# A fifth resident group of image rows, in the room of offset weights, half of the beside weights and one accumulator

## The chip, the cores and the metric

The kernel runs on one core of one Trainium2 chip. The metric is device time of one execution, in microseconds; lower is better. Three runs of the kernel before took 4093.18, 4094.98 and 4102.82 us; their median is 4094.98 us.

## The reference

The input `x` has two images of 256 channels and 128 x 128 points, in f32. Two layers follow each other, each added to its input:

1. `x1 = x + deform_conv(gn(x))`. `gn` is a group normalisation over groups of 8 channels. A 3x3 convolution of `gn(x)` gives 27 values at each point: for each of the nine taps an offset in y, an offset in x and a mask (after a sigmoid). Each tap is sampled at its shifted position by bilinear interpolation of four corners, multiplied by its mask, and the nine samples are contracted with `w_conv` (256 x 256 x 9), plus a bias.
2. `out = x1 + sum over 8 experts of p_e * conv_3x1(conv_1x3(gn(x1)))`. Each expert has 8 hidden channels, so together there are 64 hidden channels; the expert's probability is folded into the hidden values.

```
y0 = floor(py); x0 = floor(px); wy = py - y0; wx = px - x0
v00 * (1 - wy) * (1 - wx) + v01 * (1 - wy) * wx + v10 * wy * (1 - wx) + v11 * wy * wx
```

## The kernel before, in words

**Tables.** For each image a table in device memory holds normalised `x` with points as rows. One row of 4096 bytes at a point's address covers all four corners of an interpolation, because a cell holds two neighbouring rows of the image. Sampling one tap for one row of 128 points is then one gather of 128 such rows.

**Units and slots.** The middle of the program, the stream, is a sequence of 2304 units, 1152 for each image (`UPI`): 16 groups of 8 rows (`GR`), two chunks of 4 rows each, 9 taps, 4 rows. A loop over slots writes the order by hand. Slot `s` issues, for different units: the gather of unit `s + 15` (`GA`, POOL's queue), the product of unit `s + 3` (ScalarE: corner 1 times its weight into an accumulator, L564), the three remaining corners (VectorE, L570), the convolution matmul of unit `s - 8` (TensorE, L595), two transposes of unit `s - 1` (L580) and, in every second slot, the copy of two transposed units out of PSUM (`keep`, ScalarE, L588). Everything else is a piece put at a slot of its own with `put(slot, piece)`. A group is 72 slots. Engines work through their own instructions in this order, and SP's DMAs also go out in order: a DMA that waits for a buffer holds up those behind it.

**Groups of x.** A group is a tile of [128, 2, 1024] f32. Image tiles live in three buffers used in rotation (`XB`, pool `x`) and in `XR` = 4 further ones (pool `x_stay`). `x_tile` (L278) chooses: the last `XR` groups of an image, and the first `XR` of image 0, take the latter. `stays` (L285) says which groups keep their result in SBUF for the second layer: the last `XR` of image 0, the last `XR + XB` of image 1. The results of other groups are stored to `x1` (L611) and read back by the experts (L726). `load_x` (L531) loads group g + 1 at slot 72 g - 54, in the case of image 0 only from the group on that the head has not kept.

**Head.** All 16 groups of image 0 are loaded, their statistics taken, and its table is written. Groups 0 to `XB + XR - 1` stay in SBUF. `offset_pieces` (L206) then makes the weights of the offset convolution with the normalisation folded in: `wus` is `wu` times 1/deviation; `spread`, two matmuls and nine shifted matmuls give the constants of the shift; `at` holds base positions for the first, the middle and the last group. There is one set of `wus` and of the three `at` for each image.

**Stream, image 0.** Beside the units, `table_beside` (L614) makes image 1's table. A first pass reads image 1 for statistics: one chunk (512 KB) every 10 slots, and the last `XR` groups as whole tiles in `x_stay`, each when the group of image 0 that held the buffer has been stored. Norm pieces and image 1's `offset_pieces` follow. A second pass goes backwards over the 32 chunks: load unless still resident (L623, L627), normalise (ScalarE, L654), transpose, copy, and store 1 MB of table rows (L203). Its step is 21 slots; a load stands 20 slots ahead of its normalise. `offsets_of` (L300) computes gather indices and weights of each group some 83 slots ahead of its first unit.

**Stream, image 1.** The second layer for image 0 (`experts`, L710) runs beside image 1's units, one chunk every 33 slots, from the last chunk backwards. **Tail:** the second layer for image 1, 16 groups from the last backwards, nothing beside it.

**Second layer.** `back` (L757) multiplies hidden rows that pair up in the 128 partitions, with two of the four slots of `wout`; `back_beside` (L767) uses half of the partitions of the two other slots, whose other halves are zero.

**Accumulators.** The product's accumulators come from a pool of 9 (`acc`, L510).

Of the kernel before, what the change touches and what calls it, by code (L numbers as in the profile page):

```python
# [31 lines left out]
F32 = mybir.dt.float32  # L32
I32 = mybir.dt.int32
AF = mybir.ActivationFunctionType
ALU = mybir.AluOpType
# [3 lines left out]
P = 128  # L39
B, C, H, W = 2, 256, 128, 128  # L40
NH = C // P
# [3 lines left out]
NO = 3 * K2  # L45
NX = 3 * NO
NU = 3 * NX
# [3 lines left out]
GR = 8  # L51
# [6 lines left out]
ER = 64  # L58
# [3 lines left out]
UPG = UPC * CPG  # L62
UPI = UPG * NG
UNITS = B * UPI
GA = 15
# [1 line left out]
TL = 1  # L67
KL = 2
LM = 8
XB, XR = 3, 4  # L70


@with_exitstack
def layers(ctx, tc, x, w_om, b_om, w_cv, b_cv, w_in, w_out, probs, out):
    nc = tc.nc
# [5 lines left out]
    cp = ctx.enter_context(tc.tile_pool(name="const", bufs=1))  # L81
# [7 lines left out]
    idp = cp.tile([P, P + 2], F32, name="idp")  # L89
# [19 lines left out]
    base = cp.tile([P, GR, NO], F32, name="base")  # L109
# [13 lines left out]
    bias = cp.tile([P, NO], F32, name="bias")  # L123
    bcv = cp.tile([P, NH], F32, name="bcv")
    pr = cp.tile([P, 1], F32, name="pr")
    wu = cp.tile([P, NH, 3, 3, NO], F32, name="wu")
    win = cp.tile([P, NH, 3, ER], F32, name="win")

    wout = cp.tile([P, 4, C], F32, name="wout")
    nc.gpsimd.memset(wout, 0.0)  # L130
    wcv = cp.tile([P, NH, K2, C], F32, name="wcv")

    def frame(b):
# [69 lines left out]
        nc.sync.dma_start(cells(b, y + r, n), pairs)  # L203


    def offset_pieces(norm, oc, psum, tag, name):  # L206
        mean, rstd, shift = norm
        wus = oc.tile([P, NH, 3, NX], F32, name=f"wus_{name}")
        at = [oc.tile([P, GR, NO], F32, name=f"at{i}_{name}") for i in range(3)]
        spread = oc.tile([P, NH, P], F32, tag="spread", name=f"spread_{name}")  # L210
        nb = oc.tile([P, NU], F32, tag="nb", name=f"nb_{name}")
        by_row = oc.tile([P, 3, NO], F32, tag="by_row", name=f"by_row_{name}")
        ps = {}

        def scale(h):
            w = wu[:, h].rearrange("p y x o -> p (y x o)")
            nc.vector.tensor_scalar(
                wus[:, h].rearrange("p y o -> p (y o)"), w, rstd[:, h : h + 1], None, ALU.mult
            )

        def spread_out():
            nc.vector.tensor_copy(spread, shift.unsqueeze(2).broadcast_to([P, NH, P]))

        def constant():
            ps[0] = psum.tile([P, 512], F32, tag=tag, name=f"ps_nb_{name}")
            for h in range(NH):
                nc.tensor.matmul(
                    ps[0][:, :NU], lhsT=spread[:, h], rhs=wu[:, h].rearrange("p y x o -> p (y x o)"),
                    start=(h == 0), stop=(h == NH - 1),
                )  # L230

        def shifted():
            ps[1] = psum.tile([P, 512], F32, tag=tag, name=f"ps_at_{name}")
            for ty in range(3):
                for tx in range(3):
                    at_ = (2 - ty) * NX + tx * NO
                    nc.tensor.matmul(
                        ps[1][:, ty * NO : (ty + 1) * NO], lhsT=idp[:, tx : tx + P],
                        rhs=nb[:, at_ : at_ + NO], start=(tx == 0), stop=(tx == 2),
                    )  # L240

        def rows(t):
            return by_row[:, t].unsqueeze(1).broadcast_to([P, GR, NO])

        pieces = [
            lambda: scale(0),
            lambda: scale(1),
            spread_out,
            constant,
            lambda: nc.vector.tensor_copy(nb, ps[0][:, :NU]),  # L250
            shifted,
            lambda: nc.vector.tensor_copy(
                by_row.rearrange("p t o -> p (t o)"), ps[1][:, : 3 * NO]
            ),
            lambda: nc.vector.tensor_tensor(
                at[1], base, bias.unsqueeze(1).broadcast_to([P, GR, NO]), ALU.add
            ),
            lambda: nc.vector.tensor_tensor(at[1], at[1], rows(0), ALU.add),
            lambda: nc.vector.tensor_tensor(at[1], at[1], rows(1), ALU.add),
            lambda: nc.vector.tensor_tensor(at[1], at[1], rows(2), ALU.add),  # L260

            lambda: nc.vector.tensor_copy(at[0], at[1]),
            lambda: nc.vector.tensor_copy(at[2], at[1]),
            lambda: nc.vector.tensor_sub(at[0][:, 0], at[0][:, 0], by_row[:, 0]),
            lambda: nc.vector.tensor_sub(at[2][:, GR - 1], at[2][:, GR - 1], by_row[:, 2]),
        ]
        return (wus, at), pieces

    def pool(stack, name, bufs, **kw):
        return stack.enter_context(tc.tile_pool(name=name, bufs=bufs, reuse_waits="tile", **kw))  # L270
# [17 lines left out]
    stream = ExitStack()  # L288
# [4 lines left out]
    p_m = pool(stream, "p_m", 3, space=PSUM)  # L293
    norms0, offs = [None] * B, [None] * B
# [125 lines left out]
    with ExitStack() as s:  # L420
# [24 lines left out]
        nc.sync.dma_start(bcv, b_cv)  # L445
        nc.sync.dma_start(wcv, w_cv)
        nc.sync.dma_start(win, w_in)
        for i, (even, odd) in enumerate(((1, 2), (None, 0), (0, 1), (2, None))):
            for half, t in enumerate((even, odd)):
                if t is not None:  # L450
                    nc.sync.dma_start(wout[half * ER : (half + 1) * ER, i], w_out[:, t])
        for half in range(2):
            nc.sync.dma_start(pr[half * ER : (half + 1) * ER], probs)
        for b in range(B):
# [4 lines left out]
        mean, rstd, shift = norms0[0]  # L459
# [20 lines left out]
        for g in range(NG):  # L480
# [4 lines left out]
            for i in range(0, GR, 2):  # L485
                ps = ht.tile([P, 2, C], F32, tag="t", name=f"hpt_{g}_{i}")
# [20 lines left out]


    gp = pool(stream, "gather", GA)
    ap = pool(stream, "acc", 9)  # L510
    sp = pool(stream, "sampled", 3)
    st = pool(stream, "stat", 1)
    p_o = pool(stream, "p_o", 1, space=PSUM)
    p_t = pool(stream, "p_t", 3, space=PSUM)
    oc = pool(stream, "offs", 1)
    offs[0], pieces = offset_pieces(norms0[0], oc, p_m, "m", "0")
    for piece in pieces:
        piece()
    sides = ExitStack()
    stream.enter_context(sides)  # L520
# [5 lines left out]
    def put(slot, piece, opens=False):  # L526
        sched[slot].append(piece)
        if opens:
            opened.add(slot)
# [84 lines left out]
    def table_beside(b):  # L614
        xq = pool(sides, "tx", 2)
        pq = pool(sides, "tpx", 2)
        held = {}
# [3 lines left out]
        def load(j, what):  # L621
            held[what, j] = xq.tile([P, NH, N], F32, tag="tx", name=f"{what}_{b}_{j}")
            nc.sync.dma_start(held[what, j], xv[:, :, j * N : (j + 1) * N])  # L623

        def load_group(g, what):
            xt = held[what, "g", g] = x_tile(b, g, what)
            nc.sync.dma_start(xt, xv[:, :, g * GN : (g + 1) * GN])  # L627
            if g < XB:
                xts[b, g] = xt
# [41 lines left out]
        slot = 4  # L671
        for j in range(NCH):
            g, i = divmod(j, CPG)
            if g < NG - XR:
                put(slot, lambda j=j: load(j, "xs"))
            elif i == 0:

                slot = max(slot, UPG * (g - NG + XR + 1) + LM + 12)
# [6 lines left out]
        for piece in pieces:  # L685
            put(slot, piece)
            slot += 2
        offs[b], pieces = offset_pieces(norms0[b], oc, p_m, "m", str(b))
        for n, piece in enumerate(pieces):
            put(slot + 2 * n, piece)  # L690
        slot -= 12
        for j in range(NCH - 1, -1, -1):
            g, i = divmod(j, CPG)
            if g < XB and i == CPG - 1:
                put(slot, lambda g=g: load_group(g, "xt"))
            elif XB <= g < NG - XR:
                put(slot, lambda j=j: load(j, "xt"))
            for h in range(NH):
                put(slot + 20 + 3 * h, lambda j=j, h=h: normalise(j, h))
            put(slot + 24, lambda j=j: start(j))  # L700
            for n, i in enumerate(range(0, CR, 2)):
                put(slot + 26 + 4 * n, lambda j=j, i=i: turn_rows(j, i))
                put(slot + 28 + 4 * n, lambda j=j, i=i: keep_rows(j, i))
            put(slot + 33, lambda j=j: store_cells(b, CR * j, held["px", j], 0, CR))
            slot += 21
        put(slot + 13, store_top)
        return slot + 14

# [1 line left out]
    def experts(b, norm, pools, psums, put_, rows, order, first, step, ahead, early=0):  # L710
# [3 lines left out]
        xs, ns, hs, ps = {}, {}, {}, {}  # L714
        _, rstd, shift = norm
        n, nj = rows * W, rows // 2
# [50 lines left out]
        def back_beside(ci):  # L767


            own, edge = slice(0, (nj - 1) * W), slice((nj - 1) * W, nj * W)  # L770
            low, rest = slice(0, W), slice(W, nj * W)
            parts = [(0, ci, rest, own), (1, ci, own, rest), (0, ci - 1, low, edge), (1, ci + 1, edge, low)]
            parts = [part for part in parts if 0 <= part[1] < count]
            for m in range(NH):
                for i, (t, c, to, of) in enumerate(parts):
                    half = slice(ER, P) if t == 0 else slice(0, ER)
                    nc.tensor.matmul(  # L777
                        ps[t][:, m, to], lhsT=wout[half, 1 + 2 * t, m * P : (m + 1) * P],
                        rhs=hs[c][half, of], start=False,
                        stop=(banks or m == NH - 1) and all(part[0] != t for part in parts[i + 1 :]),  # L780
                    )
# [14 lines left out]
        for i in range(count + 1):  # L796
            e = first + step * i
# [7 lines left out]
            if i > 0:  # L805
# [4 lines left out]
                at_ = e + 22  # L810
# [15 lines left out]
    for G in range(B * NG):  # L826
        b, g = divmod(G, NG)
        slot = UPG * G
# [12 lines left out]
    slot = UPI + LM + 10  # L841
# [18 lines left out]
    while s < end or any(t >= s for t in sched):  # L860
# [9 lines left out]
        if when(s - LM):  # L870
            u = s - LM
            apply_tap(u)
            b, ci, k, i = unit(u)
            if k == K2 - 1 and i % NH == NH - 1:
                m = i // NH
# [69 lines left out]
```

## Time and profile before

| | us |
|---|---|
| median of the runs | 4094.98 |
| the profiled execution's own time | 3743.08 |
| its span, first to last instruction | 3741.3 |
| stream of image 0, about | 156 to 1895 |
| second pass of image 1's table, first to last store issued | 745 to 1739 |
| stream of image 1, about | 1895 to 3550 |
| tail, to the end | 3550 to 3741 |

One execution was profiled; all views are of it. It is 352 us shorter than the median of the runs. Busy time of an engine is a sum over its instructions; the granted clock of TensorE is given as a share of full speed, and its mean is 0.980. A group's row reads: line, engine, operation, output <- inputs, shapes, count, busy us and mean ns of one, then the idle time ahead of these instructions and what ended most of it.

### The profile page before, as it was taken

Reading aid. Unit: us, or ns where it says so; the run is one execution under the profiler, and the core shown is the slowest. Engines: PE = TensorE matmul, PEld = TensorE weight load, DVE = VectorE, ACT = ScalarE, POOL = GpSimd, SP = SyncE. Lnnn points to the kernel's source line nnn. Section 1 sums busy time; section 2 is a strip of 40 time slices with the busy share of each in tenths; the row PEclk is TensorE's granted clock in tenths of the full one; section 3 lists DMA queues with packets and bytes.
Section 4 is the critical chain, followed back from the end, with each engine's and each line's share of the span. In section 5 each row is a group of like instructions: output and inputs, shape, how many; then the busy total and the mean of one; then the engine's idle time right before and its main releaser. Section 6 shows DMA issues by size and latency. Waiting matters only on the chain. (4 is left out here: it accounts for less than half of the span.)

```text
span 3741.3 us, 51320 instructions
## 1 busy us (share of the span) xinstructions
PE 3379.1 (90%) x13916; PEld 1799.5 (48%) x13916; DVE 3354.6 (90%) x7922; ACT 1918.1 (51%) x3883; POOL 2381.9 (64%) x2337
## 2 busy tenths in 40 slices
PE   3688889999888888889999999999999999999999
PEld 2444444444444444444444555555555555555433
DVE  6499999999888889899999999999999999999812
ACT  2355544555555555555555555555555555555432
POOL 0377666667666667667777766777777677776400
PEclk9699999999999999999999999999999999999999
DMA  9999999999999999999999999999999999999743
GB/s 358 376 407 405 399 400 390 379 395 412 406 400 410 409 406 396 410 397 398 395 390 393 400 387 410 400 403 403 399 407 403 400 409 392 409 404 387 294 150 120
DMA packets 421960, 1431.71 MB, mean 383 GB/s; under 512 B 41726, under 2 KB 45482, under 8 KB 421546
## 3 DMA queue, kind: packets, MB, share of 16 engines
q0 software_dynamic: 331776, 1208.11, 82.0%
q1 hardware_dynamic: 89898, 220.33, 15.4%
q8 instruction: 113, 1.85, 0.2%
q14 instruction: 173, 1.42, 0.1%
HBM read 1302.40 MB, written 125.87 MB: 382 GB/s over the span
## 5 line engine op out<-in xcount | busy, mean ns | idle before, releaser
L570 DVE SCALAR_TENSOR_TENSOR acc<-g,wt,acc 128x256 f32<-128x256 f32 x6912 | 2966.7, 481 | 151.4 <-ACT acc L564 82.7
L554 POOL DMA_INDIRECT g<-table,cidx x2304 | 2371.0, 1029 | 1007.6 <-DVE acc L570 391.9
L595 PE MATMUL po<-sm,wcv 128*128 128x512 f32 x4608 | 2404.5, 604 | 162.6 <-ACT sm L588 84.0
L564 ACT ACTIVATE acc<-g,wt 128x256 f32<-128x256 f32 x2304 | 1120.3, 507 | 806.4 <-DMA g<-table,cidx 656.2
L580 PEld LDWEIGHTS ptr<-idp,acc 128*128 128x128 f32 x4608 | 607.2, 142 | 1459.7 <-issue 726.1
L588 ACT COPY sm<-ptr 128x512 f32<-128x512 f32 x1152 | 664.8, 577 | 728.7 <-PE ptr L580 727.0
L580 PE MATMUL ptr<-idp,acc 128*128 128x128 f32 x4608 | 909.1, 279 | 92.9 <-DVE acc L570 71.7
L595 PEld LDWEIGHTS po<-sm,wcv 128*128 128x128 f32 x4608 | 725.5, 192 | 221.8 <-ACT sm L588 112.4
L321 PE MATMUL pu<-wus,x 128*128 128x81 f32 (+2 forms) x1448 | 261.0, 306 | 0.0
L321 PEld LDWEIGHTS pu<-wus,x 128*128 128x128 f32 x1448 | 208.5, 193 | 1.9
L748 PE MATMUL ph<-xcn,win 128*64 128x254 f32 (+3 forms) x1152 | 177.8, 458 | 3.1 <-ACT xcn L731 3.1
L762 PE MATMUL pe<-h,wout 128*128 128x256 f32 (+1 forms) x384 | 125.5, 456 | 1.1 <-DVE xc L786 1.1
L786 DVE TENSOR_TENSOR xc<-pe,xc 128x512 f32<-128x512 f32 x84 | 55.1, 684 | 73.2 <-issue 70.8
L748 PEld LDWEIGHTS ph<-xcn,win 128*64 128x64 f32 x1152 | 79.0, 138 | 81.3 <-issue 51.5
L755 ACT ACTIVATE h<-ph,pr 128x256 f32<-128x256 f32 (+1 forms) x48 | 26.3, 547 | 138.2 <-PE ph L748 138.1
L604 DVE SCALAR_TENSOR_TENSOR x<-po,bcv,x 128x512 f32<-128x512 f32 x116 | 86.6, 747 | 8.1 <-PE po L595 8.1
L786 DVE TENSOR_TENSOR x<-pe,x 128x512 f32<-128x512 f32 x44 | 28.3, 683 | 71.7 <-PE pe L777 71.7
L762 PEld LDWEIGHTS pe<-h,wout 128*128 128x128 f32 x384 | 66.8, 190 | 39.8 <-issue 36.4
L608 DVE BATCH_NORM_STATS2 stats<-x 128x6 f32<-128x512 f32 x116 | 79.7, 687 | 0.1
L491 DVE COPY hpx<-hpt 128x512 f32<-128x512 f32 x32 | 21.1, 687 | 57.0 <-DMA table<-hpx 46.0
L777 PE MATMUL pe<-h,wout 64*128 64x128 f32 (+1 forms) x752 | 69.3, 321 | 0.0
L777 PEld LDWEIGHTS pe<-h,wout 64*128 64x128 f32 x752 | 51.8, 187 | 25.6 <-issue 16.9
(102 smaller groups left out, 845.9 us busy)
## 6 DMA issues: line engine op xcount, KB each, us to landing
g<-table,cidx POOLq DMA_INDIRECT x2304, 9.3
table<-tpx SPq DMA_DIRECT2D x32, 1024.0 KB, 11.3
table<-hpx SPq DMA_DIRECT2D x15, 2048.0 KB, 9.4
x<-in_x_dram SPq DMA_DIRECT2D x29, 1024.0 KB, 12.6
out_dram<-xc SPq DMA_DIRECT2D x42, 512.0 KB, 7.7
x<-x SPq DMA_DIRECT2D x18, 1024.0 KB, 10.3
xs<-in_x_dram SPq DMA_DIRECT2D x24, 512.0 KB, 8.3
xc<-x SPq DMA_DIRECT2D x24, 512.0 KB, 8.5
```

What stands on the lines that cost most here:

```text
L321: nc.tensor.matmul(held["ps", j][:, lo:hi], lhsT=xt[:, h, r * W : (r + 1) * W], rhs=w[:, lo - i + 2 : hi - i + 2], start=(i == 2 and h == ...
L554: nc.gpsimd.indirect_dma_start(out=gt[:], out_offset=None, in_=tables[b][:, :], in_offset=bass.IndirectOffsetOnAxis(ap=idx[:, rr, k : k + ...
L564: nc.scalar.activation(acc, gts[u][:, 0:C], AF.Copy, scale=wt[:, 0, rr, k : k + 1])
L570: nc.vector.scalar_tensor_tensor(accs[u], gt[:, q * C : (q + 1) * C], wt[:, q, rr, k : k + 1], accs[u], ALU.mult, ALU.add)
L580: nc.tensor.transpose(pts[u // 2][:, h, (r % 2) * W : (r % 2 + 1) * W], acc[:, h * P : (h + 1) * P], ident)
L588: nc.scalar.copy(sms[u // CR][:, :, (r - 1) * W : (r + 1) * W], pts.pop(u // 2))
L595: nc.tensor.matmul(pos_[b, ci, m], lhsT=wcv[:, h, k, m * P : (m + 1) * P], rhs=sms[u // CR][:, h], start=(k == 0 and h == 0), stop=(k == K ...
L604: nc.vector.scalar_tensor_tensor(v, pos_.pop((b, ci, m)), bcv[:, m : m + 1], v, ALU.add, ALU.add)
L748: nc.tensor.matmul(o[:, :, to], lhsT=win[:, h, tap], rhs=pairs[:, t, :, of], start=(q == 0), stop=(q == 5),)
L762: nc.tensor.matmul(ps[t][:, m], lhsT=wout[:, 2 * t, m * P : (m + 1) * P], rhs=hs[ci], start=(banks or m == 0), stop=False,)
L777: nc.tensor.matmul(ps[t][:, m, to], lhsT=wout[half, 1 + 2 * t, m * P : (m + 1) * P], rhs=hs[c][half, of], start=False, stop=(banks or m == ...
L786: nc.vector.tensor_tensor(v, ps[t][:, ms].rearrange("p h (j x) -> p h j x", x=W), v, ALU.add)
```

## The change

`XR` becomes 5. In SBUF, four things become smaller: `wus` and the `at` tile become tiles with a tag, so that image 1's overwrite image 0's, and the first and last group's positions are made one at a time in a tile `edge`; `spread` holds one half of the channels at a time; `wout` has three slots for four (the two halves that `back_beside` reads now share one), and its memset goes; the accumulators become 8. Image 1's offset pieces move from the end of the first pass to slots from `UPI - 68 - GA - UPG + 46` = 1043 on, and its last group's `edge` to slot 1728. The second pass has a step of 20 slots instead of 21.

```diff
@@ -67,7 +67,7 @@
 TL = 1
 KL = 2
 LM = 8
-XB, XR = 3, 4
+XB, XR = 3, 5
 
 
 @with_exitstack
@@ -126,8 +126,8 @@
     wu = cp.tile([P, NH, 3, 3, NO], F32, name="wu")
     win = cp.tile([P, NH, 3, ER], F32, name="win")
 
-    wout = cp.tile([P, 4, C], F32, name="wout")
-    nc.gpsimd.memset(wout, 0.0)
+
+    wout = cp.tile([P, 3, C], F32, name="wout")
     wcv = cp.tile([P, NH, K2, C], F32, name="wcv")
 
     def frame(b):
@@ -203,68 +203,81 @@
         nc.sync.dma_start(cells(b, y + r, n), pairs)
 
 
-    def offset_pieces(norm, oc, psum, tag, name):
-        mean, rstd, shift = norm
-        wus = oc.tile([P, NH, 3, NX], F32, name=f"wus_{name}")
-        at = [oc.tile([P, GR, NO], F32, name=f"at{i}_{name}") for i in range(3)]
-        spread = oc.tile([P, NH, P], F32, tag="spread", name=f"spread_{name}")
-        nb = oc.tile([P, NU], F32, tag="nb", name=f"nb_{name}")
-        by_row = oc.tile([P, 3, NO], F32, tag="by_row", name=f"by_row_{name}")
-        ps = {}
+    def offset_pieces(b, oc, psum, tag):
+        held = {}
+
+        def tile_of(what, shape):
+            held[what] = oc.tile(shape, F32, tag=what, name=f"{what}_{b}")
+            return held[what]
 
         def scale(h):
+            if h == 0:
+                offs[b] = tile_of("wus", [P, NH, 3, NX]), [None] * 3
             w = wu[:, h].rearrange("p y x o -> p (y x o)")
             nc.vector.tensor_scalar(
-                wus[:, h].rearrange("p y o -> p (y o)"), w, rstd[:, h : h + 1], None, ALU.mult
-            )
-
-        def spread_out():
-            nc.vector.tensor_copy(spread, shift.unsqueeze(2).broadcast_to([P, NH, P]))
-
-        def constant():
-            ps[0] = psum.tile([P, 512], F32, tag=tag, name=f"ps_nb_{name}")
-            for h in range(NH):
-                nc.tensor.matmul(
-                    ps[0][:, :NU], lhsT=spread[:, h], rhs=wu[:, h].rearrange("p y x o -> p (y x o)"),
-                    start=(h == 0), stop=(h == NH - 1),
-                )
+                held["wus"][:, h].rearrange("p y o -> p (y o)"), w, norms0[b][1][:, h : h + 1],
+                None, ALU.mult,
+            )
+
+        def spread_out(h):
+            shift = norms0[b][2][:, h : h + 1]
+            nc.vector.tensor_copy(tile_of("spread", [P, P]), shift.broadcast_to([P, P]))
+
+        def constant(h):
+            if h == 0:
+                held["ps"] = psum.tile([P, 512], F32, tag=tag, name=f"ps_nb_{b}")
+            nc.tensor.matmul(
+                held["ps"][:, :NU], lhsT=held["spread"], rhs=wu[:, h].rearrange("p y x o -> p (y x o)"),
+                start=(h == 0), stop=(h == NH - 1),
+            )
 
         def shifted():
-            ps[1] = psum.tile([P, 512], F32, tag=tag, name=f"ps_at_{name}")
+            ps = held["ps"] = psum.tile([P, 512], F32, tag=tag, name=f"ps_at_{b}")
             for ty in range(3):
                 for tx in range(3):
                     at_ = (2 - ty) * NX + tx * NO
                     nc.tensor.matmul(
-                        ps[1][:, ty * NO : (ty + 1) * NO], lhsT=idp[:, tx : tx + P],
-                        rhs=nb[:, at_ : at_ + NO], start=(tx == 0), stop=(tx == 2),
+                        ps[:, ty * NO : (ty + 1) * NO], lhsT=idp[:, tx : tx + P],
+                        rhs=held["nb"][:, at_ : at_ + NO], start=(tx == 0), stop=(tx == 2),
                     )
 
-        def rows(t):
-            return by_row[:, t].unsqueeze(1).broadcast_to([P, GR, NO])
+        def rows_out():
+            nc.vector.tensor_copy(
+                tile_of("by_row", [P, 3, NO]).rearrange("p t o -> p (t o)"), held["ps"][:, : 3 * NO]
+            )
+
+        def begin():
+            offs[b][1][1] = tile_of("at", [P, GR, NO])
+            nc.vector.tensor_tensor(
+                held["at"], base, bias.unsqueeze(1).broadcast_to([P, GR, NO]), ALU.add
+            )
+
+        def add_row(t):
+            row = held["by_row"][:, t].unsqueeze(1).broadcast_to([P, GR, NO])
+            nc.vector.tensor_tensor(held["at"], held["at"], row, ALU.add)
+
+        def edge(t, r):
+
+            e = offs[b][1][t] = tile_of("edge", [P, GR, NO])
+            nc.vector.tensor_copy(e, held["at"])
+            nc.vector.tensor_sub(e[:, r], e[:, r], held["by_row"][:, t])
 
         pieces = [
             lambda: scale(0),
             lambda: scale(1),
-            spread_out,
-            constant,
-            lambda: nc.vector.tensor_copy(nb, ps[0][:, :NU]),
+            lambda: spread_out(0),
+            lambda: constant(0),
+            lambda: spread_out(1),
+            lambda: constant(1),
+            lambda: nc.vector.tensor_copy(tile_of("nb", [P, NU]), held["ps"][:, :NU]),
             shifted,
-            lambda: nc.vector.tensor_copy(
-                by_row.rearrange("p t o -> p (t o)"), ps[1][:, : 3 * NO]
-            ),
-            lambda: nc.vector.tensor_tensor(
-                at[1], base, bias.unsqueeze(1).broadcast_to([P, GR, NO]), ALU.add
-            ),
-            lambda: nc.vector.tensor_tensor(at[1], at[1], rows(0), ALU.add),
-            lambda: nc.vector.tensor_tensor(at[1], at[1], rows(1), ALU.add),
-            lambda: nc.vector.tensor_tensor(at[1], at[1], rows(2), ALU.add),
-
-            lambda: nc.vector.tensor_copy(at[0], at[1]),
-            lambda: nc.vector.tensor_copy(at[2], at[1]),
-            lambda: nc.vector.tensor_sub(at[0][:, 0], at[0][:, 0], by_row[:, 0]),
-            lambda: nc.vector.tensor_sub(at[2][:, GR - 1], at[2][:, GR - 1], by_row[:, 2]),
+            rows_out,
+            begin,
+            lambda: add_row(0),
+            lambda: add_row(1),
+            lambda: add_row(2),
         ]
-        return (wus, at), pieces
+        return pieces, lambda: edge(0, 0), lambda: edge(2, GR - 1)
 
     def pool(stack, name, bufs, **kw):
         return stack.enter_context(tc.tile_pool(name=name, bufs=bufs, reuse_waits="tile", **kw))
@@ -445,10 +458,9 @@
         nc.sync.dma_start(bcv, b_cv)
         nc.sync.dma_start(wcv, w_cv)
         nc.sync.dma_start(win, w_in)
-        for i, (even, odd) in enumerate(((1, 2), (None, 0), (0, 1), (2, None))):
+        for i, (even, odd) in enumerate(((1, 2), (2, 0), (0, 1))):
             for half, t in enumerate((even, odd)):
-                if t is not None:
-                    nc.sync.dma_start(wout[half * ER : (half + 1) * ER, i], w_out[:, t])
+                nc.sync.dma_start(wout[half * ER : (half + 1) * ER, i], w_out[:, t])
         for half in range(2):
             nc.sync.dma_start(pr[half * ER : (half + 1) * ER], probs)
         for b in range(B):
@@ -507,14 +519,14 @@
 
 
     gp = pool(stream, "gather", GA)
-    ap = pool(stream, "acc", 9)
+    ap = pool(stream, "acc", 8)
     sp = pool(stream, "sampled", 3)
     st = pool(stream, "stat", 1)
     p_o = pool(stream, "p_o", 1, space=PSUM)
     p_t = pool(stream, "p_t", 3, space=PSUM)
     oc = pool(stream, "offs", 1)
-    offs[0], pieces = offset_pieces(norms0[0], oc, p_m, "m", "0")
-    for piece in pieces:
+    pieces, _, last_rows = offset_pieces(0, oc, p_m, "m")
+    for piece in (*pieces, last_rows):
         piece()
     sides = ExitStack()
     stream.enter_context(sides)
@@ -685,9 +697,14 @@
         for piece in pieces:
             put(slot, piece)
             slot += 2
-        offs[b], pieces = offset_pieces(norms0[b], oc, p_m, "m", str(b))
-        for n, piece in enumerate(pieces):
-            put(slot + 2 * n, piece)
+
+        pieces, first_rows, last_rows = offset_pieces(b, oc, p_m, "m")
+        at = UPI - 68 - GA - UPG + 46
+        for n, piece in enumerate((*pieces[:2], *[None] * 3, *pieces[2:], first_rows)):
+            if piece:
+                put(at + 2 * n, piece)
+        assert at + 2 * n < UPI - 68 - GA + 55
+        put(UPI + UPI // 2, last_rows)
         slot -= 12
         for j in range(NCH - 1, -1, -1):
             g, i = divmod(j, CPG)
@@ -702,7 +719,7 @@
                 put(slot + 26 + 4 * n, lambda j=j, i=i: turn_rows(j, i))
                 put(slot + 28 + 4 * n, lambda j=j, i=i: keep_rows(j, i))
             put(slot + 33, lambda j=j: store_cells(b, CR * j, held["px", j], 0, CR))
-            slot += 21
+            slot += 20
         put(slot + 13, store_top)
         return slot + 14
 
@@ -775,7 +792,7 @@
                 for i, (t, c, to, of) in enumerate(parts):
                     half = slice(ER, P) if t == 0 else slice(0, ER)
                     nc.tensor.matmul(
-                        ps[t][:, m, to], lhsT=wout[half, 1 + 2 * t, m * P : (m + 1) * P],
+                        ps[t][:, m, to], lhsT=wout[half, 1, m * P : (m + 1) * P],
                         rhs=hs[c][half, of], start=False,
                         stop=(banks or m == NH - 1) and all(part[0] != t for part in parts[i + 1 :]),
                     )
```

## The prediction

> **What bounds the kernel now.** I read the clock first (0.980 over the span), then the busy shares, the slices, the groups, the waits by stage and the DMA issues. The page's first part and the data rows of the slices:
>
> ```profile
> PE 3379.1 (90%) x13916; PEld 1799.5 (48%) x13916; DVE 3354.6 (90%) x7922; ACT 1918.1 (51%) x3883; POOL 2381.9 (64%) x2337
> ...
> PEclk9699999999999999999999999999999999999999
> DMA  9999999999999999999999999999999999999743
> GB/s 358 376 407 405 399 400 390 379 395 412 406 400 410 409 406 396 410 397 398 395 390 393 400 387 410 400 403 403 399 407 403 400 409 392 409 404 387 294 150 120
> ```
>
> Three things are near their limit at once: VectorE, TensorE, and a DMA stream at 380 to 412 GB/s until the last four slices. Which of them ends a wait differs by stage. The groups name the unit of work, one gather and three adds, 2304 times:
>
> ```profile
> L570 DVE SCALAR_TENSOR_TENSOR acc<-g,wt,acc 128x256 f32<-128x256 f32 x6912 | 2966.7, 481 | 151.4 <-ACT acc L564 82.7
> L554 POOL DMA_INDIRECT g<-table,cidx x2304 | 2371.0, 1029 | 1007.6 <-DVE acc L570 391.9
> L564 ACT ACTIVATE acc<-g,wt 128x256 f32<-128x256 f32 x2304 | 1120.3, 507 | 806.4 <-DMA g<-table,cidx 656.2
> ```
>
> ScalarE's product (L564) waits 656 us for gathers; where this outlasts the adds, VectorE waits for ScalarE (82.7 us). The view of stretches says where (columns: window, its length, busy us of PE, PEld, DVE, ACT, POOL, clock, DMA share, GB/s):
>
> ```profile
> 175.00:620.00 445.00, 391.57 (x1429) 190.84 (x1430) 433.54 (x1025) 226.79 (x464) 312.76 (x304) 0.99 1.02 401
> 620.00:735.00 115.00, 104.90 (x400) 52.79 (x399) 112.80 (x275) 57.81 (x124) 78.82 (x79) 0.99 0.99 379
> ...
> 985.00:1735.00 750.00, 653.98 (x2533) 349.99 (x2532) 675.78 (x1612) 419.71 (x844) 512.87 (x488) 0.97 1.02 405
> 1735.00:1895.00 160.00, 147.05 (x537) 71.29 (x536) 155.35 (x376) 87.92 (x181) 119.91 (x118) 0.99 1.01 393
> 1895.00:3541.00 1646.00, 1596.07 (x6971) 874.66 (x6970) 1599.68 (x3812) 887.90 (x1863) 1159.22 (x1138) 1.00 1.01 396
> 3541.00:3742.00 201.00, 185.43 (x793) 75.04 (x791) 46.88 (x79) 49.41 (x51) 0.00 (x0) 0.97 0.36 134
> ```
>
> VectorE is 97 to 98% busy everywhere except from 985 to 1735 us, where image 1's table is written beside image 0's stream: there it is 90% busy while DMA runs at 405 GB/s. VectorE's own waits in that stretch (line, releaser, us, times, longest):
>
> ```profile
> DVE acc L570 <- ACT acc L564: 58.0, 85, 1.5
> ```
>
> With 6.5 us more from 735 to 985, that is 64.5 of the 82.7 us. So in this profiled execution the table's second pass is bound by DMA, the rest of the stream by VectorE (TensorE at 97% in image 1), and the tail by TensorE: 10.84 us from one group's totals to the next, DMA share 0.36.
>
> The runs shown are another matter. The profiled execution took 3743.08 us, the median of the runs is 4094.98, 352 us longer. The page's 1431.71 MB over 4094.98 us is 350 GB/s. Taking out the tail (201 us at 134 GB/s, 27 MB), 1404.8 MB in 4095 - 201 = 3894 us is 361 GB/s, on average, through head and stream.
>
> **What the skill says.** "HBM Reference", Specifications: a core alone measures about 425 GB/s, two cores of a pair about 358 GB/s each. The profiled 400 to 412 is of the first kind; the 361 I worked out for the runs is within 1% of the second. No trace shows the runs, so that they are bandwidth-bound is an estimate from that page and the byte count; it is the choice on which the forecast turns. "Perfetto Trace Analysis", Identifying the Most-Contended Engine: DMA is to be judged by HBM utilisation, not occupancy. This agrees with the trace, whose share is 1.02 at 396 and at 405 GB/s alike, while VectorE is held up only at the second.
>
> **The change part by part.**
>
> *Resident groups, XR 4 to 5.* A group is [128 x 2 x 1024] f32, 1.049 MB. Counted in the rows of DMA issues: the head keeps image 0's group 7, so its load at slot 378 goes; image 1's group 11 is read once for statistics and table instead of twice (xs 24 to 22 halves, 4 to 5 groups; xt 18 to 16 halves); image 0's group 11 isn't stored to x1 (12 to 11 stores) nor read back by its experts (24 to 22 halves); image 1's group 8 isn't stored (9 to 8) nor read in the tail (9 to 8). Six groups, 6.29 MB of 1431.71, 0.44%; five of them (5.24 MB) before the tail. The sixth is worth nothing: the tail's cover is TensorE's 10.84 us a group, and without it 1.049 MB is 2.6 us.
>
> *The second pass moved.* With g >= 11 the statistics' last five groups go at slots 224, 244, 264, 308, 380 (before: four, ending at 308), so the pass starts about 72 slots later; its step is 20 for 21 slots; it ends at 1084 instead of 1044. Each chunk issues the same two normalisations (809 ns), one row copy, eight transposes, two copies (579 ns) and one table store of 1.049 MB. Between the passes the light stretch grows from about 94 to 186 slots. What matters is bytes above the pace of VectorE. A slot at that pace is 1646 / 1152 = 1.43 us, in which 405 GB/s moves 579 KB; the gather is 524 KB, so 55 KB a slot is free. Before: 32 table stores, 12 MB of second reads, 9 loads and 8 stores of image 0, 61 groups = 64.0 MB, less 672 x 55 KB = 37.0: 27.0 MB too many, 66.7 us, which is what the 64.5 us of waits show. After: 32, 11, 8 and 6, 57 groups = 59.8 MB, less 640 x 55 KB = 35.2: 24.6 MB, 60.7 us. So -6 us. Image 1 adds about -1 us: its reads of x1 from 2300 us on run at 403 GB/s, and only 7.7 us of VectorE's waits lie in the whole of it.
>
> *Accumulators 9 to 8.* 0. product(u) is issued at slot u - 3 and would wait for turn(u - 8). ScalarE's own queue has by then run keep(u - 8) or keep(u - 7), which waited for that turn or a later one. No new wait; with 7 there would be one.
>
> *Offset weights shared by both images.* The pieces of image 1 go from slots 370 to 400 to slots 1043 to 1075. The writing of wus at 1043 must wait for the last row matmuls of image 0's group 15 at slot 1041. Its shifted matmuls (slots 1046, 1048, 1050) ran at 1640, 1643, 1646 us and pm (slot 1052) at 1648, so TensorE keeps step: 0, at most one wait of about 3 us in front of VectorE's adds, in a stretch where it has slack. Spread in two halves: in the head a chain spread, matmul, spread, matmul costs about 1.5 us more (a copy 0.29, two matmuls near 1 us), ending near 160 us; the first adds start at 162.5 after their gathers. Hidden; 1.5 us if the gathers were quicker. The at/edge copies: 4 to 3 of 0.27 us and 4 to 3 subtractions of 0.19: -0.5 us.
>
> *wout.* One memset less (0.94 us at 3.6 us on POOL, 42 us ahead of its next work): 0. back_beside reads the same halves.
>
> Sum in the profiled regime: -6 -1 -0.5 +0 = -7.5 us, 3743.1 to about 3736. In the regime of the runs, where I take the stream to be bound by bytes throughout, five groups count in full: 5.24 MB / 361 GB/s = -14.5 us, 4095.0 to 4080.5. I forecast 4081. A change within 0.3% (12.3 us) is what can't be told from none.
>
> **Rivals.**
> A: the runs are longer for a reason that isn't bytes (launch, a lower TensorE clock). Then only the second pass gains: -7.5 us, 4087.5; between -1 and -11. For it: VectorE is at 97% and TensorE too, and no view shows the runs. Against: 361 GB/s coincides with the skill's paired share.
> B (forecast): bound by bytes, -14.5 us.
> C: slower. The pass has two tx buffers and a fixed 20 slots from load to normalisation, 28.6 us, while its step shrinks; loads landed in a median of 14.9 us. If the denser pass pushes landing past 28.6 us, normalise stands at the head of ScalarE's queue with the products behind it, and VectorE behind those; it is paid 22 times. From 1.2 us late on, 22 x 1.2 = 26 us eats the gain and ends 12 us slower, at 4107. Against: traffic per slot in the pass rises only from 628 to 632 KB. Also at risk is the end of the table: last store at slot 1083, landing 8 slots later, first gather of image 1 at 1137; 46 slots are left.
> D: the extra buffer doesn't hold what it should (a resident group reloaded): 4095. The loads' counts exclude most of it.
>
> **How the numbers follow.** B 0.48, A 0.32, C 0.16, D 0.04. B is faster by over 0.3% but for a part at its weak end; A has as much at its strong end: faster 0.48. A and D within 0.3%: 0.36. C: 0.16. B's own range is 4074 to 4085 (-21 if the light stretch also gains, -10 if a third of the five groups falls in VectorE's cover). To hold 8 in 10 the range takes in A and the start of C: 4068 to 4104.
>
> **What would show it.** In the issues: xt x16, xs x22, xc x22 and x8, x<-x and x<-xt together 19, 1425.4 MB. In the stretches: the first table store near 850 us instead of 745, the last near 1790, and VectorE's waits for L564 in the pass at 58 to 60 us instead of 64.5. A profiled span near 3734. Wrong if the waits in the pass grow, if normalise (L654's place) waits for xt, or if POOL's first gather of image 1 waits for a table store; and B is wrong if the runs gain no more than the profile does.

## The result, and the profile after

The changed kernel took 4075.9 us (median of four runs, 4071.12 to 4085.45), the kernel before 4098.9 us beside it (4093.18 to 4105.98): 23 us less, ratio 0.994, 95% interval 0.9917 to 0.9963. Run once more later, beside the kernel before, it gave 0.9936 (0.9914 to 0.9958). A ratio is not the quotient of two medians (4075.9 / 4098.9 would be 0.9944), so medians and ratios below need not divide into each other.

The profile shown before the prediction is of an execution that took 3743 us; this one, and all but two of those below, come from conditions in which the kernel before needs some 4100 us. So the two pages must not be read against each other for the effect of the change; the trace that answers to this one is that of the unchanged kernel run again, the first experiment. The page after, first the busy shares and slices:

```profile
span 4083.7 us, 51328 instructions
...
PE 3494.8 (86%) x13916; PEld 1852.4 (45%) x13916; DVE 3354.7 (82%) x7922; ACT 1844.2 (45%) x3883; POOL 2306.5 (56%) x2336
...
DMA  9999999999999999999999999999999999999833
GB/s 360 368 375 380 361 368 354 359 345 382 372 391 405 396 408 385 378 403 357 333 337 348 343 334 347 353 354 355 361 367 357 340 346 364 357 326 338 303 129 124
...
L582 DVE SCALAR_TENSOR_TENSOR acc<-g,wt,acc 128x256 f32<-128x256 f32 x6912 | 2964.3, 481 | 414.8 <-ACT acc L576 266.3
...
L600 ACT COPY sm<-ptr 128x512 f32<-128x512 f32 x1152 | 673.8, 585 | 1815.4 <-PE ptr L592 1139.4
...
L576 ACT ACTIVATE acc<-g,wt 128x256 f32<-128x256 f32 x2304 | 1065.3, 508 | 51.4 <-DMA g<-table,cidx 40.2
```

VectorE's work is what it was (3354.7 us for 3354.6), an add still takes 481 ns, but its idle time before the adds is 415 us here and was 151 us in the first profile. DMA isn't at one level: it moves 372 to 408 GB/s while the table is written, and 326 to 367 in image 1 until its last slice. And the waits have changed place. The products (L576, formerly L564) wait 40 us for gathers, not 656; ScalarE's idle time now stands ahead of the copies out of PSUM (L600, formerly L588), 1815 us of it, put down mostly to TensorE.

For the long waits that attribution needs a closer look. Here is ScalarE alone in the timeline, for some 14 us of image 1, and below it the last of TensorE's transposes that the first copy after the wait reads:

```profile
2593.72 0.91 ACT L576 ACTIVATE acc<-g,wt 128x256 f32<-128x256 f32 x2
2604.72 0.59 ACT L600 COPY sm<-ptr 128x512 f32<-128x512 f32 x1 [10.09 <-PE po L607]
2605.20 0.91 ACT L576 ACTIVATE acc<-g,wt 128x256 f32<-128x256 f32 x2
2606.01 0.57 ACT L600 COPY sm<-ptr 128x512 f32<-128x512 f32 x1
2606.48 0.91 ACT L576 ACTIVATE acc<-g,wt 128x256 f32<-128x256 f32 x2
2607.29 0.57 ACT L600 COPY sm<-ptr 128x512 f32<-128x512 f32 x1
...
2597.18 0.38 PE L592 MATMUL ptr<-idp,acc 128*128 128x128 f32 x2
```

ScalarE stands still for 10 us and then works through copies and products without a gap. The last transposes that the first of these copies reads stand in the trace as ended at 2597.56, 7 us earlier. I call this a halt. Counted in the trace, from 165 to 3850 us, ScalarE is idle for over 4 us at a time 130 times, 817 us together; in the first profile's stream once, for 4.05 us.

What ends a halt stands in the trace's record of semaphore updates, which no view prints. A semaphore is a counter by which one engine tells another that a piece of work is done. All 130 halts are in front of an instruction that waits for TensorE's semaphore, and in 123 of them an update of it stands at most 0.15 us before ScalarE goes on. In the halt shown, updates stand at 2604.64, 2604.73, 2604.78, 2604.89 and 2604.93 us: five in 0.3 us, where a pair of transposes alone takes 0.38 us, so they can't have come one by one as the work ended. Three within 0.3 us occur 257 times in this stream and never in the first profile's. So ScalarE is held until TensorE's signal comes, and these signals come bunched, and late by the ends that the profile gives. Whether TensorE's work was late as well can't be told, because those ends are modelled. The trace also has holes here that the first profile's doesn't have: 3687 updates of VectorE's semaphore for 6045. Why the signals are late stays open.

The gathers are not late: putting DMA's small closing packets down to the gathers in order, in image 1 the last one of a gather ends a median of 5.8 us after its issue (first profile: 7.1), and its product starts 10.4 us after that (4.2).

What the change does to DMA is as counted. From the issues:

```profile
DMA packets 419512, 1425.42 MB, mean 349 GB/s; under 512 B 41582, under 2 KB 45338, under 8 KB 419098
...
xs<-in_x_dram SPq DMA_DIRECT2D x22, 512.0 KB
xc<-x SPq DMA_DIRECT2D x22, 512.0 KB
...
xt<-in_x_dram SPq DMA_DIRECT2D x16, 512.0 KB
xc<-x SPq DMA_DIRECT2D x8, 1024.0 KB
```

### The profile page after: what moved, and what is told of

The parts are those of the page before. It is cut to its first block, busy times and chain, and to the rows that moved or that the text cites. A ratio compares the mean times of both kernels' runs of the same rounds, so it can differ in the third digit from the quotient of the medians.

```text
span 4083.7 us, 51328 instructions
## 1 busy us (share of the span) xinstructions
PE 3494.8 (86%) x13916; PEld 1852.4 (45%) x13916; DVE 3354.7 (82%) x7922; ACT 1844.2 (45%) x3883; POOL 2306.5 (56%) x2336
## 5 line engine op out<-in xcount | busy, mean ns | idle before, releaser
L566 POOL DMA_INDIRECT g<-table,cidx x2304 | 2296.6, 997 | 1423.6 <-DVE acc L582 496.5
L607 PE MATMUL po<-sm,wcv 128*128 128x512 f32 x4608 | 2475.6, 620 | 287.5 <-issue 119.4
L600 ACT COPY sm<-ptr 128x512 f32<-128x512 f32 x1152 | 673.8, 585 | 1815.4 <-PE ptr L592 1139.4
L592 PEld LDWEIGHTS ptr<-idp,acc 128*128 128x128 f32 x4608 | 622.8, 145 | 1566.4 <-issue 1042.1
L576 ACT ACTIVATE acc<-g,wt 128x256 f32<-128x256 f32 x2304 | 1065.3, 508 | 51.4 <-DMA g<-table,cidx 40.2
L592 PE MATMUL ptr<-idp,acc 128*128 128x128 f32 x4608 | 929.2, 284 | 157.3 <-DVE acc L582 57.7
L607 PEld LDWEIGHTS po<-sm,wcv 128*128 128x128 f32 x4608 | 745.6, 197 | 355.6 <-issue 162.8
L765 PE MATMUL ph<-xcn,win 128*64 128x254 f32 (+3 forms) x1152 | 194.4, 482 | 11.5 <-issue 8.2
L616 DVE SCALAR_TENSOR_TENSOR x<-po,bcv,x 128x512 f32<-128x512 f32 x116 | 86.5, 746 | 48.2 <-remote 22.8
L349 PE MATMUL om<-u,idp 128*128 128x216 f32 x192 | 53.8, 362 | 17.4 <-ACT u L343 13.3
```

Source lines behind the costliest of these rows:

```text
L566: nc.gpsimd.indirect_dma_start(out=gt[:], out_offset=None, in_=tables[b][:, :], in_offset=bass.IndirectOffsetOnAxis(ap=idx[:, rr, k : k + ...
L576: nc.scalar.activation(acc, gts[u][:, 0:C], AF.Copy, scale=wt[:, 0, rr, k : k + 1])
L592: nc.tensor.transpose(pts[u // 2][:, h, (r % 2) * W : (r % 2 + 1) * W], acc[:, h * P : (h + 1) * P], ident)
L600: nc.scalar.copy(sms[u // CR][:, :, (r - 1) * W : (r + 1) * W], pts.pop(u // 2))
L607: nc.tensor.matmul(pos_[b, ci, m], lhsT=wcv[:, h, k, m * P : (m + 1) * P], rhs=sms[u // CR][:, h], start=(k == 0 and h == 0), stop=(k == K ...
L616: nc.vector.scalar_tensor_tensor(v, pos_.pop((b, ci, m)), bcv[:, m : m + 1], v, ALU.add, ALU.add)
```

## The experiments

Line numbers are those of each kernel. "Room" means everything of the change but the fifth group. Ratios are to the kernel before, beside each other on one chip. All in one table first; the first eleven rows are from chips where the kernel before needs about 4100 us (5 and 12; for the row "changed" the chip isn't known), the last two from one where it needs 3741 us (chip 2).

| kernel | median us | ratio | 95% interval |
|---|---|---|---|
| before, unchanged | 4096.89 | 0.9996 | 0.9983 to 1.0008 |
| 8 accumulators alone | 4100.91 | 0.9989 | 0.9968 to 1.0009 |
| room alone | 4090.71 | 0.9977 | 0.9962 to 0.9993 |
| room, 16.8 MB more | 4090.12 | 0.9975 | 0.9962 to 0.9988 |
| room, later pass | 4086.91 | 0.9962 | 0.9946 to 0.9978 |
| changed, bytes back | 4080.96 | 0.9948 | 0.9928 to 0.9967 |
| changed, bytes back, again | 4084.25 | 0.9941 | 0.9919 to 0.9964 |
| changed, step 21 | 4080.66 | 0.9948 | 0.9927 to 0.9969 |
| changed | 4075.9 | 0.994 | 0.9917 to 0.9963 |
| changed, again | 4089.32 | 0.9936 | 0.9914 to 0.9958 |
| room, products 6 ahead | 4222.34 | 1.0277 | 1.0247 to 1.0308 |
| room, 17 gather buffers | 3739.79 | 0.9996 | 0.9988 to 1.0005 |
| changed, products 2 ahead | 3732.24 | 0.9976 | 0.9967 to 0.9985 |

### The kernel before, again

No edit.

> The kernel before, unchanged, for a trace beside the others and as a measure of what the comparison can tell. Every theory: ratio 1.000, at most 0.002 from it; some 4099 us. If the runs are bound by bytes, its GB/s in the stretches should stand at one level, near 360, in both images; if not, the extra 350 us over the profiled 3743 should show as waits in places that have little to do with traffic.

4096.89 us, 0.9996: with this many runs the comparison can tell some 0.0013, with fewer less. Its trace (span 4077.8 us) decides the first question. The stretches (window, its length, busy us of PE, PEld, DVE, ACT, POOL, clock, DMA share, GB/s; the first is image 0 before the second pass, the second lies in that pass, the third in image 1):

```profile
175.00:620.00 445.00, 365.46 (x1304) 180.16 (x1304) 397.69 (x941) 194.86 (x427) 275.50 (x280) 0.95 0.98 370
1000.00:1700.00 700.00, 596.04 (x2235) 316.73 (x2233) 594.36 (x1429) 352.68 (x748) 427.35 (x431) 0.93 1.00 387
2100.00:3800.00 1700.00, 1530.44 (x6467) 828.87 (x6468) 1466.93 (x3484) 788.53 (x1711) 1034.13 (x1050) 0.97 0.95 354
```

387 GB/s in the pass and 354 in image 1, where VectorE is busy 86% of the time: no ceiling of bandwidth at 361. And the waits of this unchanged kernel already look like those of the changed one:

```profile
ACT sm L588 <- PE ptr L580: 1091.1, 622, 8.5
...
ACT sm L588 <- remote: 444.9, 92, 11.6
...
DVE acc L570 <- ACT acc L564: 211.5, 69, 7.1
...
L570 DVE SCALAR_TENSOR_TENSOR acc<-g,wt,acc 128x256 f32<-128x256 f32 x6912 | 2962.7, 480 | 401.8 <-ACT acc L564 211.5
```

ScalarE halts for over 4 us 126 times, 809 us in all, and 122 of the halts end with an update of TensorE's semaphore. VectorE is idle for 485 us of this stream (151 us in the first profile), 362 of them during a halt or within 2 us of its end. So most of the 350 us between the first profile and the runs comes with these halts, as far as VectorE can't work on through them; they belong to the conditions of the run, not to the change. TensorE's mean clock is 0.948 instead of 0.980.

### The room alone, and the bytes put back

The room alone is the changed kernel with four groups and the old step:

```diff
-XB, XR = 3, 5
+XB, XR = 3, 4
...
-            slot += 20
+            slot += 21
```

> Everything of the change but the fifth group: XR stays 4 and the step 21; the shared offset weights, three slots of wout and 8 accumulators are in. Bytes theory (five groups fewer make the gain): ratio 1.000 to 1.001, some 4099 us. Schedule theory (the later and shorter second pass makes it): 1.000 too, as the pass is where it was. Room theory (8 accumulators or the shared weights make the gain): 0.994, some 4076 us.

4090.71 us, 0.9977. Neither of the values expected (1.000 or 0.994): the room without a single byte less is worth some 9 us, two fifths of the gain. The other side of the same cut, five tiles but the traffic of four:

```diff
+XU = 4
...
-        return g >= NG - XR - (XB if b == B - 1 else 0)
+        return g >= NG - XU - (XB if b == B - 1 else 0)
...
+        elif (b, g) != (0, XB + XU):
+            return
...
-            v = place(j, "xs" if g >= NG - XR else "xt")
+            v = place(j, "xs" if g >= NG - XU else "xt")
...
-            elif XB <= g < NG - XR:
+            elif XB <= g < NG - XU:
```

> The changed kernel with all six groups of traffic put back where the kernel before has them: group 7 of image 0 is loaded once more, group 11 of image 1 is read a second time for the table, group 11 of image 0 and group 8 of image 1 go to x1 and are read back. Five tiles, the second pass 72 slots later and its step of 20 stay. Bytes theory: the gain goes, ratio 0.998 to 1.000, 4091 to 4099 us. Schedule and room theories: it stays, 0.994, some 4076 us.

4080.96 us, 0.9948; the gain stays. Its trace counts 1431.71 MB again, as before the change:

```profile
DMA packets 421688, 1431.71 MB, mean 351 GB/s; under 512 B 41710, under 2 KB 45466, under 8 KB 421274
```

Repeated with the changed kernel beside it:

> The changed kernel once more, beside the kernel before. Chips of two kinds have been seen: some on which the kernel before takes 4100 us and ScalarE halts, one on which it takes 3741 us as in the first profile. On the first kind: 0.994 to 0.995. On the second kind, bytes theory with the second pass bound by DMA (the prediction's sum, 7.5 us): 0.998, some 3734 us. If products one slot later made what the run with them gained there: 1.000.

> The changed kernel with all six groups of traffic put back, once more. On a chip where the kernel before takes 4100 us: 0.995, as it was, bytes being worth nothing there. On one where it takes 3741 us, bytes theory: at least three quarters of the gain goes, 0.9995 to 1.000, some 3740 us; schedule theory: it stays, 0.998.

0.9936 and 0.9941. Over both pairs (0.9948 against the changed kernel's 0.994, and this one) the bytes are worth 0.0006 with an uncertainty of about 0.002, where the forecast's 14.5 us would be 0.0035.

### More bytes

The same question with a larger lever, on the room alone: one group more read in each of 16 groups of image 1.

```diff
+    more = pool(stream, "more", 1)
+
+    def load_more(g):
+        xt = more.tile([P, NH, GN], F32, tag="more", name=f"more_{g}")
+        nc.sync.dma_start(xt, view(x, 1)[:, :, g * GN : (g + 1) * GN])
...
+        if b == 1:
+            put(slot + 30, lambda g=g: load_more(g))
```

> The room alone, with one more load of a group (1.049 MB) in each of the 16 groups of image 1's stream, into a tile that nobody reads: 16.8 MB more. Bytes theory, at 361 GB/s: 46 us more than the room alone, some 4137 us, 1.009. Pause theory (in the runs ScalarE halts for 4 to 12 us ahead of its copies out of PSUM with all inputs there, and DMA has room in image 1): 0 to 6 us more, 4090 to 4097 us, 0.998 to 0.9995.

4090.12 us, 0.9975, for the room's 4090.71 and 0.9977. 16.8 MB cost nothing that can be told. Image 1 in this trace against the unchanged kernel's 354 GB/s:

```profile
2100.00:3800.00 1700.00, 1528.71 (x6425) 830.65 (x6424) 1452.82 (x3450) 780.96 (x1693) 1026.94 (x1040) 0.96 0.96 360
```

DMA simply moves more, 360 GB/s. This settles that the runs' stream in image 1 isn't bound by bytes.

### The schedule of the second pass

The changed kernel with the old step:

```diff
-            slot += 20
+            slot += 21
```

> The changed kernel with the second pass at its old step of 21 slots; it then ends at slot 1116 instead of 1084. Bytes and room theories: 0.994, within 0.002 of the changed kernel, some 4076 us. Schedule theory: part of the gain goes, or more comes: 0.991 or 0.997.

0.9948: the step by itself makes no difference that can be told. The room with the pass put where the change has it:

```diff
-        slot += 18
+        slot += 18 + UPG
...
-            slot += 21
+            slot += 20
```

> The room alone (four resident groups), with the second pass put where the changed kernel has it: 72 slots later and a step of 20. Schedule theory (the later pass makes what the room does not): 0.995, some 4079 us. If the fifth tile is needed for another reason: 0.998, some 4090 us, as the room alone.

4086.91 us, 0.9962 (0.9946 to 0.9978), between the room's 0.9977 and the changed kernel's 0.994, and not clearly apart from either. The later pass may make half of what the fifth group adds to the room, or none.

### The accumulators

The kernel before with one line changed:

```diff
-    ap = pool(stream, "acc", 9)
+    ap = pool(stream, "acc", 8)
```

> The kernel before with 8 accumulators for 9 and nothing else. By the prediction's own step (no new wait, since ScalarE's queue has already waited for that transpose): 1.000, some 4099 us. If the 9 us that the room alone gave came from the accumulators: 0.998, some 4090 us. A rival, that one accumulator less costs: 1.001 or more.

0.9989 (0.9968 to 1.0009): no cost. The interval takes in 1 and the room's 0.9977, so whether the accumulator gives nothing or all of the room's 9 us can't be told.

### What the halts are

If ScalarE halts for reasons of its own, more products in hand should let VectorE work on. On the room alone:

```diff
-LP = 3
+LP = 6
...
-    ap = pool(stream, "acc", 8)
+    ap = pool(stream, "acc", 12)
```

> The room alone, with the product 6 slots ahead of its unit for 3, and 12 accumulators for 8 (4 KB). VectorE then has three more units, some 4.3 us of work, ready when ScalarE halts; a gather has 9 slots for 12 before its product. Pause theory: of about 125 halts of over 4 us most lose up to 4.3 us less, 100 to 300 us less, 3800 to 4000 us, 0.93 to 0.975. Bytes theory: no change to the room alone, 0.998, some 4090 us, or slower where gathers now come late for their products.

4222.34 us, 1.0277: 132 us slower than the room alone. That is against the pause theory; the bytes theory had allowed for "slower" without a figure. Its waits:

```profile
ACT sm L600 <- PE ptr L592: 931.2, 625, 6.8
ACT sm L600 <- remote: 644.5, 100, 14.2
...
DVE x L616 <- PE po L607: 171.0, 43, 11.5
```

The halts are 119, about as many, but the longest grow to 14 us, and now VectorE's residual (L616) waits for the convolution, 171 us (11.1 in the changed kernel). A product further ahead also has its gather three slots less ahead. So a new theory: ScalarE halts on gathers whose completion reaches it late, and lead is what counts. Two tests of it:

```diff
-GA = 15
+GA = 17
```

> The room alone (four resident groups), with its free 8 KB in two more gather buffers: 17 for 15, so a gather may be issued 14 slots ahead of its product for 12. Lead theory (what ScalarE halts for are gathers whose completion reaches it late; the run with products 6 ahead lost three slots of lead and 132 us): 30 to 90 us less than the room alone, 4000 to 4060 us, 0.977 to 0.992. Theory of ScalarE's own halts: no change to the room alone, 0.9977, some 4090 us.

```diff
-LP = 3
+LP = 2
```

> The changed kernel with the product 2 slots ahead of its unit for 3, so that a gather has 13 slots for 12 and VectorE one unit less in hand. Lead theory: 10 to 45 us less than the changed kernel, 0.983 to 0.992. Theory of ScalarE's own halts: some 125 halts of over 4 us with 1.4 us less cover each, up to 180 us more, 1.00 to 1.04.

These two ran on a chip where the kernel before takes 3741.14 us. Each has only five waits of ScalarE of over 4 us in its stream, none over 4.5 us, so they say nothing on the lead. The room with 17 gather buffers changes nothing there (0.9996), so the room alone is probably worth nothing there either.

The semaphore updates speak against the lead theory, and also against halts of ScalarE's own. In the run with products 6 ahead, 111 of the 119 halts end at most 0.15 us after an update of TensorE's semaphore, and so do 46 of the 48 waits of over 2 us in front of L616 (230 us together). What ScalarE and VectorE wait for there is TensorE's signal. Why it costs more with products further ahead is not shown.

The second of them, though, shows the changed kernel, but for one product, in the conditions in which the prediction's sum was made. 3732.24 us, 8.9 less than the kernel before. Its first table store and its last, VectorE's waits in its pass from 840 to 1800 us, and the stretches of pass and image 1:

```profile
L203 SPq DMA_DIRECT2D table<-tpx x32: 359/366/369, 843.6 to 1785.7; - x32
```

```profile
DVE acc L582 <- ACT acc L576: 56.5, 88, 2.0
```

```profile
840.00:1800.00 960.00, 851.53 (x3301) 436.77 (x3300) 879.87 (x2111) 544.93 (x1099) 660.13 (x630) 0.99 1.02 405
...
1890.00:3531.00 1641.00, 1591.34 (x6959) 871.61 (x6958) 1596.92 (x3807) 874.82 (x1861) 1148.12 (x1135) 1.00 1.01 395
```

The wait of the same kind in the first profile's pass, from 735 to 1735 us:

```profile
DVE acc L570 <- ACT acc L564: 64.5, 96, 1.5
```

8.0 us less waiting at the same 405 GB/s. From unit 180 to unit 1152 it takes 1453.6 us for the first profile's 1463.4, and for image 1 1.5 us less. The run with 17 gather buffers, which lacks the fifth group, helps to read this: it takes 1461.3 us from unit 180 to unit 1152, so the gain of the pass shows against it too, but for image 1 it takes 1646.8 us to the 1646.9 us here.

## Why the prediction was right or wrong

The forecast, faster by 14.5 us, has the direction, and the measured 4075.9 us lie in its range. The mechanism behind the number fell, so it is right for a wrong reason, by luck.

**Wrong: the choice of regime.** The step that failed is "In the regime of the runs, where I take the stream to be bound by bytes throughout, five groups count in full". The 361 GB/s was an average over time that contained halts, and it met the 358 GB/s of the Trainium skill's "HBM Reference", Specifications, by coincidence. The unchanged kernel's trace shows 387 GB/s in the pass and 354 in image 1; bytes taken out and put back change nothing that can be told; 16.8 MB more cost nothing. The page's two figures may be right; no run here has reached a limit at 358. What the prediction missed could have been asked of it: a stream that is bound by bytes throughout has to show one level in all its stages, and one profile of another execution can't show it. Its own sign for this mechanism, "B is wrong if the runs gain no more than the profile does", did not catch it: the runs gained 23 us and the program with products 2 ahead 8.9 us where it needs 3741 us, and yet it was not the bytes. Rival A had the right reason, that the runs are longer for something other than bytes, but its -7.5 us is not what they gained.

**Right, where it applied: the sum of the second pass.** -6 us in the pass was forecast for the profiled conditions, with a span near 3734. The run with products 2 ahead has 3731.7, waits of 56.5 instead of 64.5 us (forecast: 58 to 60), and table stores from 843.6 to 1785.7 us (forecast: near 850 and 1790). It differs from the changed kernel in one more line, so this is strong but not clean. The -1 us of image 1 is not shown, since the run without the fifth group takes the same time there. Two readings in the prediction are a little off, without effect on its sum: VectorE is 95% busy, not 97 to 98%, from 735 to 985 us, and the DMA share at 396 GB/s is 1.01, not 1.02.

**Wrong: the room at nothing.** The prediction put the shared weights, wout and the accumulators at 0 to -0.5 us. In the runs' conditions they gave about 9 (0.9977 and 0.9975 in two runs with the same schedule). For the accumulators alone, 0.9989 agrees with the prediction's 0 but doesn't exclude the 9 us. In the single profiles, image 0 (units 0 to 1152) took 1856 and 1867 us in the two kernels with the old offset weights, and 1834 to 1851 in eight with the new ones; image 1 took 1857 and 1874 us, and 1864 to 1884. This points to image 0's stream, where the moved pieces are, but doesn't show it: each figure is of one execution, and the eight scatter by 17 us. Whether the gain comes from these pieces, or from the addresses that the smaller tiles move, wasn't tried. For the halts' regime no view had been there to price it.

**Not mentioned: the rest.** The fifth tile without its bytes and the later pass together give another 0.003 (0.9948 against the room's 0.9977). No effect of the step could be told; the later pass may be half of it. This stays open, and with it the cause of most of the 23 us. That DMA's counts would be 1425.4 MB, that no wait for the table's end and no late normalise (rival C) would appear, was right.

## What to carry to other kernels

When the runs are far from the profiled execution, the gap itself is the first thing to explain, and an average rate that happens to fit a known ceiling is no explanation: ask whether the rate is the same in stages of different traffic, and test it with added bytes, which is cheap. Before a wait is called an engine's own, look when the semaphore that it waits for was updated. To credit a saving of bytes, put back the bytes and keep the rest of the change; here the room made for a buffer was worth 0.0023, and the traffic that the buffer saved 0.0006 with an uncertainty of 0.002.

## What the runs showed of the hardware

- The same unchanged program takes 3741 us on one chip (2) and 4100 us on two others (5 and 12), with the same busy time of VectorE (3354.6 us in the first profile, 3356.4 us in the trace of some 4080 us), the same head (163 us to the first add) and tail (201 to 202 us). The difference comes with halts of ScalarE of 4 to 12 us in the stream, 126 of them in the unchanged kernel and 130 in the changed one. 122 and 123 of these end at most 0.15 us after an update of TensorE's semaphore. Such updates come in bunches there, three within 0.3 us 232 and 257 times, and never in the first profile. Why was not found.
- In traces with halts the profile's releaser has to be read with care: it names TensorE for a copy whose transposes stand as ended 7 us before, and "remote" for 392 to 645 us. The time of the semaphore's update tells when the wait ended, and not the end of the work that is named.
- Products three slots further ahead of their use, with 12 accumulators for 8 and their gathers three slots less ahead, cost 132 us in those conditions.
